# A scan's output product, made by the full array or by its four quarters

## The chip, the cores and the metric

The kernel runs on one core of a Trainium2 chip. The metric is the device time of one launch in microseconds (us), the median of several runs. A profile of one execution shows the engines: PE (matmul), PEld (its weight loads), DVE, ACT, POOL and SP (which here only issues DMAs).

## The reference

Four layers over an image x of 1024 channels and 64x64 places, each added to its input after a normalization over groups of channels:

```python
x = x + L0(gn(x))      # layernorm, decays from a softplus, a causal sum over channels
x = x + W1 @ gn(x) + b1
x = x + L2(gn(x))      # the scan layer
x = x + W3 @ gn(x) + b3
```

The change lies in the third layer. Its core is a selective scan over N = 4096 tokens in two heads, each with 512 channels and 8 states, each in an order of its own:

```python
perm = argsort(score of the token's place)              # one order per head
h_t = exp(dt_t * A) * h_{t-1} + dt_t * B_t * x_t        # 8 states x 512 channels
y_t = C_t . h_t + D * x_t
y = y put back into the order of the image
out = silu(Wo @ (y * silu(gate) + res))
```

## The kernel before

All arithmetic is f32. The large products (1024x1024 weights) are made by Strassen's method: sums and differences of blocks of the image (tiles t and b, lines 514 and 942) and of the weights (lines 471 to 495) are multiplied at line 984 into tiles mm.

The scan goes in chunks. A chunk holds both heads: partitions 0 to 63 are head 0, 64 to 127 head 1. Of the 64 rows of a head the first 8 are its states, the other 56 are tokens in scan order. So 74 chunks (NK) hold 4096 tokens. Token rows lie in DRAM (tok_d, 512 channels and 130 columns of dt, B and C). For chunk k:

- gather (line 1467, POOL): an indirect DMA brings 128 rows into rows[k] by the indices src, five chunks ahead.
- turn_rows (lines 1481 and 1482, PE): turns B, C and the sums of dt into the PSUM tile pr, one bank of the tag tp, which has two banks.
- spread_decay (lines 1488 to 1496, DVE): reads pr and makes the decays E and the operands cd and bts. Line 1496 is the last that reads pr.
- line 1560 (ACT): the exponential of E.
- cross (line 1503, PE): pg, the products of B and C. weigh (lines 1511 to 1516, DVE): from E and pg the matrix G, 128x128, of which only two diagonal blocks of 64x64, one for each head, are ever written; the rest is zero.
- apply (line 1520, PE): py = G^T rows[k], one product of 128x128 by 512 columns into the bank of tag y. Then ACT copies the 8 state rows of each head into the first rows of rows[k+1] (line 1523, two copies) and the whole of py over rows[k] (line 1525).
- scatter (line 1529, POOL): an indirect DMA writes the 128 rows of 512 channels to y_rows in DRAM by the indices dst. State rows and the rows beyond 4096 go to spare rows at the end.

In the same stage PE makes the products for res (line 984, function run), which lie between the steps of the scan: short steps hold 8 passes of them, long ones 16. ACT and DVE take their results from PSUM (lines 1173, 1177, 1185), ACT fills the image tiles for them (line 514), POOL makes differences of tiles (line 942) and sums of the last layer's weights.

The order of instructions on PE, DVE, ACT and POOL in this stage is that of the program (a manual schedule); only SP's order is left to the scheduler. The loop is:

```python
for k in range(-1, NK + 1):
    gather(k + 5); turned = turn_rows(k + 1); spread_decay(k + 1, *turned)
    next_units(upto)                 # products for res
    y = apply(k - 1); weigh(k, cross(k))
    exp(E of k + 1); step_sums(k + 3)
    scatter(k - 1, y)
    next_units(upto); next(sums)
```

The indices come from a sorting network that runs on DVE earlier, in the stage before (near 884 us). Its end (lines 402 to 414) writes the order to perm_d and reads it back, transposed, into src and dst, with POOL issuing the DMAs (lines 404, 410, 412). The rows of dst for states and spare rows are a constant, column "to", copied at line 232. After the scan, load_y (line 1677) reads y_rows for the output product.

Of the kernel before, what the change touches and what calls it, by code (L numbers as in the profile page):

```python
# [10 lines left out]
F32 = mybir.dt.float32  # L11
BF16 = mybir.dt.bfloat16
I32 = mybir.dt.int32
F32R = mybir.dt.float32r
AF = mybir.ActivationFunctionType
ALU = mybir.AluOpType
# [4 lines left out]
P = 128  # L21
C = 1024
HW = 64
N = HW * HW
CT = C // P
NB = 8
FB = N // NB
TPB = FB // P
NT = N // P
R = FB // HW  # L30
HEADS, S, DH = 2, 8, 512
# [4 lines left out]
LC = P // HEADS  # L36
# [38 lines left out]
        ("Alog", S), ("D", 1), ("mob", 4 * HEADS), ("dbcb", HEADS * NF)]  # L75

_CST = [("ident", P), ("fold", LC), ("same", P), ("upto", LC), ("far", LC), ("eye", LC), ("eye8", S),
        ("from", 1), ("to", NK), ("group", P), ("row", TR), ("rows", P),
        ("gx", NT), ("gy", NT), ("flip", 7)]


# [13 lines left out]
def tile_net(ctx: ExitStack, tc: tile.TileContext, x, par_d, cst_d, w_d, w2_d, dbcw_d, out):  # L95
# [19 lines left out]
    tok_d = dram.tile([HEADS * N + NSPEC, DH + NF2], F32, name="tok_d")  # L115
    y_d = nc.dram_tensor("y_rows", (HEADS * N + P * NK, DH), F32, kind="Internal").ap()
    perm_d = dram.tile([HEADS * N, 1], I32, name="perm_d")


    cst = const.tile([P, NCST], F32, name="cst")  # L120
# [102 lines left out]


    src = const.tile([P, NK], I32, name="src")
    dst_ = const.tile([P, NK], I32, name="dst")
    diag = const.tile([P, LC], F32, name="diag")

    def prepare_scan():

        nc.vector.tensor_copy(src, cst[:, CST["from"]].to_broadcast([P, NK]))
        nc.vector.tensor_copy(dst_, cst[:, CST["to"]])
        nc.vector.tensor_scalar(diag, cst[:, CST["eye"]], pcol("D", 0), None, ALU.mult)
        rows = sum1.tile([NSPEC, DH + NF2], F32, name="spec", bufs=1)
        nc.gpsimd.memset(rows, 0.0)
        for at in (BF, CF):
            for j in range(KW // HS)[HI[at]]:
                c = DH + at + j * HS
                nc.gpsimd.tensor_copy(rows[:HS, c : c + HS], ident[:HS, :HS])
        nc.sync.dma_start(tok_d[HEADS * N :, :], rows)  # L240
# [5 lines left out]
    turned_ = [sorts.tile([P, 2, HEADS * NT], F32, name=f"turned{i}") for i in range(2)]  # L246
    swap = [sorts.tile([P, 2, P // 2], F32, name=f"swap{i}") for i in range(2)]
    order_i = sorts.tile([HEADS * NT, P], I32, name="order_i")
    nc.gpsimd.iota(order_i, pattern=[[1, P]], base=0, channel_multiplier=P)

    def make_scores():
# [76 lines left out]
    def sort_work():  # L328

        eng, bits = nc.vector, 7
        flip = cst[: HEADS * NT, CST["flip"]]

        def compare(t, new, bit):
            def two(x):
                v = x.rearrange("p (u s l) -> p u s l", s=2, l=2 ** bit)
                return v[:, :, 0], v[:, :, 1]

            rows, _, w = t.shape
            a, b = two(t.rearrange("p c w -> p (c w)"))
            (ka, kb), (ia, ib) = two(t[:, 0]), two(t[:, 1])
            (ka2, kb2), (ia2, ib2) = two(new[:, 0]), two(new[:, 1])
            over = swap[0][:rows, :, : w // 2]
            same = swap[1][:rows, 0, : w // 2]
            step = swap[1][:rows, 1, : w // 2]
            def like(x):
                return x.rearrange("p (u l) -> p u l", l=2 ** bit)
            for i, (x, y) in enumerate(((ka, kb), (ia, ib))):  # L350
                eng.tensor_tensor(like(over[:, i]), x, y, ALU.is_gt)
            eng.tensor_tensor(like(same), ka, kb, ALU.is_equal)
            eng.tensor_tensor(same, same, over[:, 1], ALU.mult)
            eng.tensor_tensor(ka2, ka, kb, ALU.min)
            eng.tensor_tensor(same, same, over[:, 0], ALU.add)
            eng.tensor_tensor(like(step), ib, ia, ALU.subtract)
            eng.tensor_tensor(kb2, ka, kb, ALU.max)
            eng.tensor_tensor(step, step, same, ALU.mult)
            eng.tensor_tensor(ia2, ia, like(step), ALU.add)
            eng.tensor_tensor(ib2, ib, like(step), ALU.subtract)  # L360

        def negate(v):
            eng.tensor_scalar(v, v, -1.0, None, ALU.mult)

        def turn_over(t, new):
            rows, _, w = t.shape
            yield "turn"
            pt = ps_tp("sort")
            for c in range(2):
                nc.tensor.transpose(pt[:w, c * rows : (c + 1) * rows], t[:, c], ident[:rows, :rows])  # L370
            yield "take"
            nc.scalar.copy(new.rearrange("p c w -> p (c w)"), pt[:w, : 2 * rows])

        now, other = lines
        negate(now.rearrange("p c (u s l) -> p (c u) s l", s=2, l=2)[:, :, 1])
        for k in range(1, 13):
            if k > bits:
                t, t2 = turned_
                if k == bits + 2:
                    yield "take"  # L380
                yield from turn_over(now, t)
                for bit in reversed(range(k - bits)):
                    yield "compare"
                    compare(t, t2, bit)
                    t, t2 = t2, t
                yield from turn_over(t, now)
            for bit in reversed(range(min(k, bits))):
                yield "compare"
                compare(now, other, bit)
                now, other = other, now  # L390
            if k + 1 < bits:
                v = now.rearrange("p c (u t s l) -> p (c u) t s l", t=2, s=2, l=2 ** k)
                negate(v[:, :, 0, 1])
                negate(v[:, :, 1, 0])
            elif k + 1 == bits:
                v = now.rearrange("p c (s l) -> p c s l", s=2)
                for s in range(2):
                    eng.tensor_scalar(v[:, :, s], v[:, :, s], flip[:, s : s + 1], None, ALU.mult)
            elif k < 12:
                i = k - bits + 2  # L400
                eng.tensor_scalar(now, now, flip[:, i : i + 1], None, ALU.mult)
        eng.tensor_copy(order_i, now[:, 1])
        yield "take"
        nc.gpsimd.dma_start(perm_d.rearrange("(a p) o -> a (p o)", p=P), order_i)
        yield "take"
        for h in range(HEADS):
            r0, full = h * LC + S, (NK - 1) * LT
            perm = perm_d[h * N : (h + 1) * N]
            for idx in (src, dst_):
                nc.gpsimd.dma_start(idx[r0 : r0 + LT, : NK - 1],  # L410
                                  perm[:full].rearrange("(k r) o -> r (k o)", r=LT))
                nc.gpsimd.dma_start(idx[r0 : r0 + N - full, NK - 1 :], perm[full:])
# [1039 lines left out]
    with tc.tile_pool(name="l2g", bufs=8) as pgat, tc.tile_pool(name="l2b", bufs=2) as pb, tc.tile_pool(name="l2r2", bufs=4) as prg, tc.tile_pool(name="l2h", bufs=1) as ph, \  # L1452
# [7 lines left out]
        eye8 = cst[:KW, CST["eye8"]]  # L1460
        turn = cst[:, CST["ident"].start : CST["fold"].stop]
        rows, decay_, steps_ = {}, {}, {}
        y_views = dram_disjoint_views(y_d[:, :], 4)

        def gather(k):
            rows[k] = g = pgat.tile([P, DH + NF2], F32, tag="g", name=f"g{k}")
# [49 lines left out]
                nc.vector.tensor_tensor(G2[k % 2][at, at], K[at], diag[at], ALU.add)  # L1516

        def apply(k):
            py = psb.tile([P, FB], F32, tag="y", name=f"py{k}")
            nc.tensor.matmul(py, G2[k % 2], rows[k][:, :DH], start=True, stop=True)  # L1520
            if k + 1 < NK:
                for h in range(HEADS):
                    nc.scalar.copy(rows[k + 1][h * LC : h * LC + S, :DH], py[h * LC : h * LC + S])  # L1523
            y = rows.pop(k)[:, :DH]
            nc.scalar.copy(y, py)  # L1525
            return y

        def scatter(k, y):
            nc.gpsimd.indirect_dma_start(  # L1529
                out=y_views[k % len(y_views)][:, :], out_offset=bass.IndirectOffsetOnAxis(ap=dst_[:, k : k + 1], axis=0),  # L1530
                in_=y, in_offset=None,
            )

        sums = (None for _ in sum_weights2(W3, ph, nc.sync, 64, (2, 2, 1, 2, 1)))

# [396 lines left out]
def _constants():  # L1932
    c = np.zeros((P, NCST), np.float32)
    p, j = np.arange(P)[:, None], np.arange(P)[None, :]
    c[:, CST["ident"]] = p == j
    h, r = np.divmod(p, LC)
    t = np.arange(LC)[None, :]
    c[:, CST["fold"]] = r == t
    c[:, CST["same"]] = h == j // LC
    c[:, CST["upto"]] = (t < S) | (r <= t)  # L1940
    c[:, CST["far"]] = np.where((r >= S) & (t >= S) & (t < r), FAR, 0)
    c[:, CST["eye"]] = (r == t) & (r >= S)
    c[:KW, CST["eye8"]] = np.tile(np.eye(S), (KW // S, 1))
    c[:, CST["from"]] = HEADS * N + np.where(r < S, h * S + r, HEADS * S)
    c[:, CST["to"]] = HEADS * N + np.arange(NK)[None, :] * P + p
    c[:, CST["group"]] = (p // 32 == j // 32) / 32
    c[:, CST["row"]] = p // TW == j[:, :TR]
    c[:, CST["rows"]] = p % TR == j // TW
    s = 1 - 2 * ((np.arange(P)[:, None] >> np.arange(6)[None, :]) & 1)
    s[:, 5] = 1  # L1950
    c[:, CST["flip"]] = np.concatenate([s[:, :1], -s[:, :1], s[:, :5] * s[:, 1:]], axis=1)
    lin = _side()
    c[:, CST["gx"]] = np.tile(lin, HW).reshape(NT, P).T
    c[:, CST["gy"]] = np.repeat(lin, HW).reshape(NT, P).T
    return c
# [63 lines left out]
```

## Time and profile before

| | |
|---|---|
| time, median of 3 runs | 2605.09 us (2603.36 to 2606.09) |
| the profiled execution: its time | 2604.14 us |
| the profiled execution: its span | 2602.4 us, mean granted clock 0.998 |
| PE busy | 2539.4 us, 98% of the span |
| ACT busy, POOL busy | 1053.9 us and 1231.7 us |
| scan, first to last py (line 1520) | 1094.3 to 1536.5 us |
| py in the scan, PE | 148 passes, 592 ns each by their records |
| state copies, ACT, line 1523 | 146, median 576 ns |
| full copies, ACT, line 1525 | 74, median 585 ns |
| scatters, POOL, line 1529 | 74, median 996 ns |

The profile's line numbers are those of the kernel before. An f32 product appears as two passes, so its count is double. A pass's record reaches from its start to the modelled end of its drain, so records of passes that follow each other overlap; the pace is read from start to start. In a timeline each row is a run of equal instructions: start, length, engine, line, operation, out<-in, count. A number in brackets is the idle time of the engine before the row and what ended it.

### The profile page before, as it was taken

The numbers are of one execution on the slowest core, as the hardware profiler recorded it, in microseconds if no ns is written. First come the engines' busy times: TensorE is split into PE (matmuls) and PEld (weight loads), VectorE is DVE, ScalarE is ACT, GpSimd is POOL, SyncE is SP. The second block draws the span as 40 slices with busy tenths as digits, with TensorE's granted clock in tenths as the row PEclk, the third lists the DMA queues.
The fourth block names the chain that finished last, engine by engine and source line by source line (L and its number), as shares of the span: only waits on it lengthen the run. The fifth ranks groups of instructions, "written<-read, shape, count | busy, mean of one in ns | idle before, by whom it ended". The sixth has DMA issues, their size and how long they took to land.

```text
span 2602.4 us, 30961 instructions
## 1 busy us (share of the span) xinstructions
PE 2539.4 (98%) x9692; PEld 1681.3 (65%) x9692; DVE 1796.5 (69%) x3754; ACT 1053.9 (40%) x1829; POOL 1231.7 (47%) x1118
## 2 busy tenths in 40 slices
PE   5989999999999999999999999999999999899999
PEld 4654444445555555545454558888888888788887
DVE  7998675565556553487878866585685775877877
ACT  4871011025555644476767562243133323321120
POOL 4643332422424231355565636575564755655444
PEclk9999999999999999999999999999999999999999
DMA  7564747664755685587678847899898898888896
GB/s 284 214 231 154 267 168 229 206 208 127 213 136 139 145 216 142 186 283 232 207 213 256 280 157 202 224 303 271 244 304 245 240 301 226 301 287 303 299 319 216
DMA packets 426998, 597.26 MB, mean 230 GB/s; under 512 B 142004, under 2 KB 210739, under 8 KB 423764
## 3 DMA queue, kind: packets, MB, share of 16 engines
q1 hardware_dynamic: 307268, 384.69, 46.9%
q10 hardware_dynamic: 91744, 136.85, 15.0%
q0 software_dynamic: 27824, 73.74, 11.8%
q8 instruction: 79, 1.29, 0.2%
q14 instruction: 83, 0.68, 0.1%
HBM read 435.12 MB, written 160.05 MB: 229 GB/s over the span
## 4 chain that ended last, share of the span: by engine, by line
PE 85%; DVE 8%; ACT 4%; DMA 1%; issue 1%; POOL 1%; SPq 0%; ACTq 0%; DVEq 0%; POOLq 0%
PE mm L984 38%; PE q_P2P L1889 6%; PE q_P3P L1889 5%; PE q_P4P L1889 5%; PE q_P6P L1889 5%; PE q_P7P L1889 5%; PE q_P5P L1889 5%; PE q_P1P L1889 5%; PE l2pt L1235 2%; PE py L1520 2%; DVE xt L685 2%; ACT b L514 1%; DVE cvp L1216 1%; DVE stats L584 1%; PE pr L1481 1%
## 5 line engine op out<-in xcount | busy, mean ns | idle before, releaser
L984 PE MATMUL mm<-t,w 128*128 128x512 f32 x1504 | 667.5, 594 | 0.0
L984 PE MATMUL mm<-b,w 128*128 128x512 f32 x1088 | 483.1, 594 | 1.6 <-ACT xs L1259 1.1
L984 PEld LDWEIGHTS mm<-t,w 128*128 128x128 f32 x1504 | 279.7, 190 | 313.7 <-issue 305.5
L984 PEld LDWEIGHTS mm<-b,w 128*128 128x128 f32 x1088 | 202.4, 190 | 232.5 <-issue 225.4
L1529 POOL DMA_INDIRECT y_rows<-g,dst x74 | 73.6, 995 | 179.8 <-ACT g L1525 163.7
L1216 DVE SCALAR_TENSOR_TENSOR cvp<-xs,par,cvp 128x512 f32<-128x512 f32 x128 | 95.3, 754 | 76.4 <-ACT cvp L1213 74.1
L1853 ACT COPY qQ<-q_P5P 128x512 f32<-128x512 f32 x48 | 28.1, 585 | 295.7 <-PE q_P5P L1889 267.6
L471 POOL TENSOR_TENSOR s<-s 128x256 f32<-128x256 f32 (+3 forms) x120 | 130.3, 1091 | 7.5
L1523 ACT COPY g<-py 8x512 f32<-8x512 f32 x146 | 83.8, 574 | 104.0 <-PE py L1520 101.1
L1267 DVE TENSOR_TENSOR xs<-mm,xs 128x512 f32<-128x512 f32 x64 | 41.8, 685 | 118.2 <-PE mm L984 118.2
L1243 POOL TENSOR_TENSOR acc<-l2xt,acc 128x136 f32<-128x136 f32 x56 | 29.2, 522 | 194.2 <-ACT l2xt L1237 187.1
L1099 DVE SCALAR_TENSOR_TENSOR image<-mm,par,image 128x512 f32<-128x512 f32 x60 | 44.0, 745 | 84.3 <-PE mm L984 84.3
L1235 PEld LDWEIGHTS l2pt<-both,cv 128*128 128x128 f32 x512 | 76.2, 190 | 35.3 <-issue 21.5
L942 POOL TENSOR_TENSOR t<-t,b 128x512 f32<-128x512 f32 x36 | 49.5, 1401 | 96.0 <-DVE t L942 92.6
L1635 POOL TENSOR_TENSOR t_t<-qt 128x512 f32<-128x512 f32 x23 | 29.6, 1288 | 133.4 <-DVE qt L1635 68.8
L1639 ACT ACTIVATE qb<-x_x_b,gn_bias,gn_r_r 128x512 f32<-128x512 f32 x64 | 48.8, 808 | 107.8 <-DVE qQ L1813 37.3
L1889 PE MATMUL q_P4P<-t_t,wq_P4P 128*128 128x256 f32 x384 | 90.9, 380 | 1.4 <-DVE qV L1861 1.4
L1861 DVE TENSOR_TENSOR qV<-q_P4P,qV 128x512 f32<-128x512 f32 x96 | 64.8, 685 | 37.7 <-PE q_P4P L1889 36.0
L1889 PE MATMUL q_P5P<-t_t,wq_P5P 128*128 128x256 f32 x384 | 90.8, 379 | 0.0
L1889 PE MATMUL q_P6P<-t_t,wq_P6P 128*128 128x256 f32 x384 | 90.7, 379 | 0.0
L1889 PE MATMUL q_P7P<-t_t,wq_P7P 128*128 128x256 f32 x384 | 90.7, 379 | 0.0
L1889 PE MATMUL q_P2P<-t_b,wq_P2P 128*128 128x256 f32 x384 | 90.7, 379 | 0.0
(471 smaller groups left out, 5923.3 us busy)
## 6 DMA issues: line engine op xcount, KB each, us to landing
w<-s_d SPq DMA_DIRECT2D x96, 512.0 KB
w<-in_w_dram SPq DMA_DIRECT2D x70, 512.0 KB
x_x_b<-x_d ACTq DMA_DIRECT2D x28, 1024.0 KB
image<-x_d SPq DMA_DIRECT2D x12, 2048.0 KB
wq_P6P<-s_d SPq DMA_DIRECT2D x84, 256.0 KB
wq_P7P<-s_d SPq DMA_DIRECT2D x84, 256.0 KB
wq_P5P<-s_d SPq DMA_DIRECT2D x84, 256.0 KB
wq_P3P<-s_d SPq DMA_DIRECT2D x84, 256.0 KB
```

What stands on the lines that cost most here:

```text
L471: eng.tensor_tensor(out, a, b, ALU.subtract)
L685: nc.vector.tensor_tensor_scan(xt, spread[h].rearrange("p t c -> p (t c)"), xt, 0.0, ALU.mult, ALU.add)
L942: eng.tensor_tensor(B[name][k], B[one][k], B[two][k], ALU.subtract)
L984: nc.tensor.matmul(to[o], w[:, k, o * P : (o + 1) * P], B[name][k], start=(fresh and k == 0), stop=(k == KH - 1), skip_group_check=True)
L1216: nc.vector.scalar_tensor_tensor(cv, xo[:, at + t : at + t + FB], pcol("dww", 3 * o + t), cv, ALU.mult, ALU.add)
L1235: nc.tensor.matmul(pt[:, q * NV : (q + 1) * NV], cv[:, (q0 + q) * P : (q0 + q + 1) * P], both[:, o, :], start=True, stop=True)
L1520: nc.tensor.matmul(py, G2[k % 2], rows[k][:, :DH], start=True, stop=True)
L1523: nc.scalar.copy(rows[k + 1][h * LC : h * LC + S, :DH], py[h * LC : h * LC + S])
L1529: nc.gpsimd.indirect_dma_start(out=y_views[k % len(y_views)][:, :], out_offset=bass.IndirectOffsetOnAxis(ap=dst_[:, k : k + 1], axis=0), i ...
L1639: made = nc.scalar.activation(tile_of(j, name)[:, k], held[j, "x", name][:, k], AF.Identity, bias=bias, scale=scale)
L1861: nc.vector.tensor_tensor(to, ps, to, ALU.add)
L1889: nc.tensor.matmul(ps[:, o, :], w[:, k, o * P : (o + 1) * P], rhs[:, k, :], start=(new and o == 0 and k == 0), stop=(k == 1), skip_group_c ...
```

## The change

The product py becomes four. For each head h and each half of the channels (side) there is a product of the 64x64 block of G with 256 columns of that head's rows. The head decides which rows of the array it uses, the side decides which columns, so the four lie in the four quarters. Head 0's output goes to py[0], the bank of tag y, head 1's to py[1], a bank of tag tp; in each, partitions 0 to 63 hold the first 256 channels and 64 to 127 the other 256. The copies follow: four of 8x256 for the states, two of 128x256 for the whole. A row that is scattered is now half a token (256 channels), and each head is scattered by itself; the indices are 2*token + side, in DRAM tables of their own (sides_d), and the spare rows come from an iota.

```diff
-dst_ = const.tile([P, NK], I32, name="dst")
+dst_ = const.tile([P, HEADS, NK], I32, name="dst")
...
-nc.vector.tensor_copy(dst_, cst[:, CST["to"]])
+nc.gpsimd.iota(dst_, pattern=[[1, HEADS], [2 * P, NK]], base=2 * HEADS * N, channel_multiplier=2)
...
 nc.gpsimd.dma_start(perm_d.rearrange("(a p) o -> a (p o)", p=P), order_i)
+for i in range(2):
+    eng.tensor_scalar(side_i[i], now[:, 1], 2.0, float(i), ALU.mult, ALU.add)
+    nc.gpsimd.dma_start(sides_d[i].rearrange("(a p) o -> a (p o)", p=P), side_i[i])
 yield "take"
 for h in range(HEADS):
-    r0, full = h * LC + S, (NK - 1) * LT
-    perm = perm_d[h * N : (h + 1) * N]
-    for idx in (src, dst_):
+    full = (NK - 1) * LT
+    for idx, d, half in ((src, perm_d, h), (dst_[:, h], sides_d[0], 0), (dst_[:, h], sides_d[1], 1)):
+        r0 = half * LC + S
+        perm = d[h * N : (h + 1) * N]
         nc.gpsimd.dma_start(idx[r0 : r0 + LT, : NK - 1],
                           perm[:full].rearrange("(k r) o -> r (k o)", r=LT))
         nc.gpsimd.dma_start(idx[r0 : r0 + N - full, NK - 1 :], perm[full:])
...
-y_views = dram_disjoint_views(y_d[:, :], 4)
+y_views = dram_disjoint_views(y_d.rearrange("r (s c) -> (r s) c", s=2), 8)
...
 def apply(k):
-    py = psb.tile([P, FB], F32, tag="y", name=f"py{k}")
-    nc.tensor.matmul(py, G2[k % 2], rows[k][:, :DH], start=True, stop=True)
+    py = psb.tile([P, FB], F32, tag="y", name=f"py{k}"), ps_tp(f"py1_{k}")
+    for side in range(2):
+        to, at = slice(side * LC, (side + 1) * LC), slice(side * QB, (side + 1) * QB)
+        for h in range(HEADS):
+            own = slice(h * LC, (h + 1) * LC)
+            nc.tensor.matmul(py[h][to, :QB], G2[k % 2][own, own], rows[k][own, at], start=True, stop=True)
     if k + 1 < NK:
         for h in range(HEADS):
-            nc.scalar.copy(rows[k + 1][h * LC : h * LC + S, :DH], py[h * LC : h * LC + S])
+            for side in range(2):
+                nc.scalar.copy(rows[k + 1][h * LC : h * LC + S, side * QB : (side + 1) * QB],
+                               py[h][side * LC : side * LC + S, :QB])
     y = rows.pop(k)[:, :DH]
-    nc.scalar.copy(y, py)
+    for h in range(HEADS):
+        nc.scalar.copy(y[:, h * QB : (h + 1) * QB], py[h][:, :QB])
     return y

 def scatter(k, y):
-    nc.gpsimd.indirect_dma_start(
-        out=y_views[k % len(y_views)][:, :], out_offset=bass.IndirectOffsetOnAxis(ap=dst_[:, k : k + 1], axis=0),
-        in_=y, in_offset=None,
-    )
+    for h in range(HEADS):
+        nc.gpsimd.indirect_dma_start(
+            out=y_views[(HEADS * k + h) % len(y_views)][:, :],
+            out_offset=bass.IndirectOffsetOnAxis(ap=dst_[:, h, k : k + 1], axis=0),
+            in_=y[:, h * QB : (h + 1) * QB], in_offset=None,
+        )
```

The column "to" is also gone from the constants, which shrink from 954 to 880 columns. In the order of instructions nothing else moves on PE, DVE, ACT and POOL: each py, each copy and each scatter is replaced where it stood. On SP one weight load goes ahead of the three stores that preceded it.

## The prediction

> **What bounds the kernel now.** I read the page first, then windows over the stage that the change touches, the waits of PE there, and the timelines of PE, DVE and ACT inside it. The page gives the whole:
>
> ```profile
> span 2602.4 us, 30961 instructions
> PE 2539.4 (98%) x9692; PEld 1681.3 (65%) x9692; DVE 1796.5 (69%) x3754; ACT 1053.9 (40%) x1829; POOL 1231.7 (47%) x1118
> ```
>
> PE is the bound on average; what a change in one stage is worth depends on the stage. The scan's 74 steps run from 1094 to 1540 us. A window inside it, and the waits of PE over it (total, times, longest, us):
>
> ```profile
> 1150.00:1200.00 50.00, 50.00 (x144) 25.15 (x142) 38.67 (x87) 31.61 (x57) 37.58 (x36) 1.00 0.73 223
> ...
> PE py L1520 <- DVE G L1516: 2.3, 3, 1.5
> PE py L1520 <- ACT g L1525: 1.6, 2, 1.4
> ```
>
> PE never stops (50.00 of 50.00, full clock); its few waits are all for this product. So PE time removed here is span removed, as long as nobody else becomes late. The timeline of PE shows one short step:
>
> ```profile
> 1320.36 1.02 PE L1520 MATMUL py<-g,G 128*128 128x512 f32 x2
> 1320.82 0.80 PE L1503 MATMUL pg<-cd,bts 66*128 66x512 f32 x1
> 1321.46 0.49 PE L1481 MATMUL pr<-cst,g 128*128 128x192 f32 x2
> 1321.79 0.33 PE L1482 MATMUL pr<-ds,cst 128*128 128x64 f32 x2
> 1321.95 3.65 PE L984 MATMUL mm<-t,w 128*128 128x512 f32 x8
> 1325.44 1.02 PE L1520 MATMUL py<-g,G 128*128 128x512 f32 x2
> ```
>
> An f32 product is two passes (x2). Records overlap, so I take start to start: a pass of 512 columns occupies PE 0.427 us (eight mm passes: 3.49, from 1321.95 to 1325.44, the first with its weights not yet loaded), so py occupies 0.854 of the 5.08 us step. 256 columns are then 0.213 a pass.
>
> **The change on PE.** Removed: 74 py of 2 passes x 0.427 = 0.854. Added: four products of 2 passes x 0.213, which is 1.71 in a row, 0.43 if all four quarters run at once. The kernel has a near relative: line 642 puts four f32 products of 256 columns side by side in four column strips.
>
> ```profile
> 64.23 1.14 PE L626 MATMUL xpt<-cst,xn 128*128 128x128 f32 x8
> 65.30 0.64 PE L642 MATMUL pd<-xt,dtm 128*32 128x256 f32 x8
> 65.86 1.13 PE L704 MATMUL pb<-image,cst 128*128 128x512 f32 x2
> ```
>
> Eight passes start and are gone in 0.56 (65.30 to 65.86), not 1.71: four do run at once. But there is a toll. The L626 passes come every 0.122 ((1.14 - 0.286)/7, 0.286 being one record), so they end at 65.21 and L642 enters 0.09 late; and the pair behind takes 1.13 where a pair in stride takes 1.02. The visit costs 0.09 + 0.56 + 0.11 = 0.77 (0.785 in most of the others), that is 0.43 of work and 0.35 of toll. The Trainium skill, "TensorEngine Tiling (Array Packing)", Key Properties, says that changing the tiling mode drains TensorE, without a figure. The same toll for a split by rows:
>
> ```profile
> 358.26 2.31 PE L984 MATMUL mm<-t,w 128*128 128x512 f32 x5
> 360.50 0.34 PE L370 MATMUL sort<-cst,lines 64*128 64x64 f32 x2
> 360.76 2.41 PE L984 MATMUL mm<-t,w 128*128 128x512 f32 x5
> ```
>
> Five passes are 2.14, so 2.50 from 358.26 to 360.76 holds 0.36 of the visit, and the 2.41 behind it (2.31 in stride) 0.10 more: 0.46 for 0.107 of work. Both kinds of split cost 0.35, so I take 0.785 for the py visit; the bounds are 0.75 and 0.85 (weights of 64 columns instead of 32). By the skill's speedup of up to four (Theoretical Speedup, same page) the sum would be 74 x (0.43 - 0.854) = -31 us; with the drain in the trace it is 74 x (0.785 - 0.854) = -5.1 us. In some ten steps PE waits at py anyway, for ACT or DVE, so 64 steps give **-4.4 us** (bounds -6.5 and 0).
>
> **ACT.** Before: two copies 8x512 and one 128x512 per step; after: four 8x256 and two 128x256. The nearest row of half width from PSUM stands last:
>
> ```profile
> 1110.38 1.50 ACT L514 ACTIVATE b<-image,gn2b_bias,gn2b_r_r 128x512 f32<-128x512 f32 x2
> 1111.79 1.15 ACT L1523 COPY g<-py 8x512 f32<-8x512 f32 x2
> 1112.96 0.58 ACT L1525 COPY g<-py 128x512 f32<-128x512 f32 x1
> ...
> L647 ACT COPY own<-pd 128x256 f32<-128x256 f32 x8 | 3.0, 379 | 1.2 <-PE pd L642 1.2
> ```
>
> Half the columns save a third only: 4 x 0.37 + 0.38 + 0.27 (the last overlaps its follower by 0.1, as now) = 2.13 against 1.68 = +0.43 us per step, 32 us in all on an ACT that is busy 312 of 446 us. In most steps py(k) comes 2.2 us after the end of the full copy L1525 of k-1, which hides it. It is not hidden where fills (L514) or activations stand ahead of the copies in ACT's queue: the starts of py at 1113.60, 1124.10, 1259.07 and 1392.28 follow the end of L1525 within 0.06; there +0.43 each. At 1240.06 and 1373.26 ACT has worked without a pause over two or three steps; there about +1.1 each. Sum 1.7 + 2.2 = **+3.9 us** (bounds 2 and 6). E (exp) comes 0.43 later too; DVE reads it 3 us afterwards.
>
> **A new wait, pr for DVE.** Head 1's output takes a bank of tag tp, which until now alternated between the pr of two steps. Now pr(k+1) always gets the bank of pr(k), and the order of instructions shows it: pr waits for DVE, which it didn't before. It must wait until line 1496, the last reader of pr(k), is done; mm, py and all else on PE queue behind it.
>
> ```profile
> 1320.54 0.67 DVE L1496 TENSOR_TENSOR cd<-pr,cst 64x512 fp32r<-64x512 f32 x1
> ...
> 1144.94 0.67 DVE L1496 TENSOR_TENSOR cd<-pr,cst 64x512 fp32r<-64x512 f32 x1
> ...
> 1144.64 0.49 PE L1481 MATMUL pr<-cst,g 128*128 128x192 f32 x2
> ```
>
> In the usual short step L1496 ends at 1321.21 and pr starts at 1321.46: 0.25 us of slack, as in nearly thirty steps. A released PE instruction starts 0.05 after the release with 0.105 of weight load uncovered (a 1.13 py behind a wait against 1.02), so 0.16 are needed and 0.18 are left once py is 0.07 shorter: no stall. But where DVE is behind, pr now starts before L1496 ends: by 0.97 at 1144.64 and 0.98 at 1279.06, 0.34 at 1210.78, 0.13 at 1095.79, 0.5 at 1133.81, 0.39 at 1284.14. Adding 0.16 gives 1.1, 1.1, 0.5, 0.3, 0.66, 0.55. The fifth only shortens the wait for G at 1143.47, the last is gone since PE is then 1.1 later and DVE has caught up. With a little for two slacks of 0.1: **+3.3 us** (bounds 1.5 and 6).
>
> **POOL and DMA.** A second scatter per step, 0.995 each: +74 us on a POOL that is busy 243 of 446 and waits 164 for ACT before scatters. Behind it in the queue stand the gathers (five steps ahead) and the differences L942 for mm; of the tightest pair, ended at 1307.15, the product begins at 1311.80 and needs the second half 2.6 us later, so 7 us of slack hide 1.4 to 3. Without that cover a late difference would stop PE by about 1.4 a time, twelve sets. The second scatter also waits for the gather two steps back; its tail is at most 9 us behind the issue, two steps are 10. The bytes are the same in rows of 1 KB instead of 2: between nothing and twice the packet time of the scatters (half of the 28% that the software queue holds of the 16 engines here); no wait of PE in this stage ends at a DMA, so I take nothing. Before the scan: two writes of the sides (0.78 each), two more index pairs (1.9 + 0.54 each), 6.5 us on POOL at 884 to 902, ahead of weight sums and acc; POOL then idles 3.5 and 3.2 us, so 0 to 3 us come through. The two DVE multiplications (near 0.2, the row of the cast L402), the iota (0.23, row L249) against the dropped cast (0.19), and 74 columns less of constants: nothing, each being paid once and for a quarter of a microsecond. Rearranged on SP: one weight load ahead of three stores; nothing. Together **+1.0 us** (0 to 4).
>
> **Sum.** -4.4 + 3.9 + 3.3 + 1.0 = +3.8 us on the profiled execution (span 2602.4, own time 2604.14, 1.7 outside the span). The median of the runs is 2605.09, one above it: 2609.
>
> **Rivals.** *B, two rounds.* The Trainium skill, "TensorE: Matmul & The Clock Gate", Part 3 (What overlaps and what doesn't), says that a weight load overlaps running products only in another row group. The two halves of one head share a row group; they would run after each other: 2 x 0.427 + 0.35 = 1.21 per visit, +0.35 x 74 = +26, the new waits then covered by the slower PE: 2632. Against: the strips of L642 share all rows and yet all eight passes fit in 0.56. *C, no packing:* the quarters aren't used at once: 1.71 + 0.35, +1.2 x 74 = +89 less some cover: 2690. Nothing in the trace speaks for it but that quarters of 64x64 are not shown. *D, the cover fails:* POOL or DMA waits reach PE, +8 to +20: 2618. *E, faster:* the drain isn't paid for quarters, because G and the products are ready early and the queue is full: the visit falls to 0.48, -27 + 8 = -19: 2586. For it: L370 in 128*64 form enters and leaves without a toll (five passes and the visit take 2.36 from 406.79 to 409.15). Against: that one has all rows and starts at column 0, and both true splits pay. The turn to faster than before lies at a visit of 0.73.
>
> **How the numbers follow.** Main case 0.78 (2602 to 2616), B 0.08, C 0.05, D 0.04, E 0.05. About 0.2%, 5.2 us, is what a measurement of this kernel can tell from no change. The main case lies around +4 with a spread of 3, so it splits into 0.42 same, 0.35 slower, 0.01 faster; B, C, D are slower, E is faster: 0.06, 0.42, 0.52. The range reaches from 2602 over D to 2622, leaving out B, C, E.
>
> **What would show it.** Right: py as 64*64 passes, eight in 0.64 and a step near 5.0; py's visit 0.78; ACT copies of 0.36 to 0.38; waits of pr for DVE near 1144 and 1279; longer py waits for ACT near 1240 and 1373. Wrong: eight passes in 1.0 or more, short steps over 5.1, or PE waits that end at POOL or a DMA.

## The result, and the profile after

The changed kernel is slower: 2621.24 us (median of 5 executions, 2620.56 to 2630.48) against 2605.09 us for the kernel before on the same chip, ratio 1.0073 with a 95% interval of 1.0062 to 1.0084. The forecast was 2609. Nine executions of it were timed in all: seven lie between 2617.8 and 2621.6 us, two at 2629.9 and 2630.5. The first profile is one of these two; where not said otherwise, the lines below are from a profile of the same kernel at 2617.8 us, taken on the chip of the second group of experiments, where before had 2605.48 us. Line numbers are those of each run's own kernel.

```profile
span 2616.0 us, 32307 instructions
...
PE 2539.8 (97%) x10136; PEld 1667.4 (64%) x10136; DVE 1797.4 (69%) x3755; ACT 1080.6 (41%) x2049; POOL 1308.8 (50%) x1199
```

PE is as busy as before (2539.4 then) in a span that is 13.6 us longer: PE does not work more, it stands still more. To find where, I followed the start of the k-th pg in both timelines. Three stretches come out:

| stretch | before | after, 2617.8 us | longer by |
|---|---|---|---|
| start to first pg | 1090.08 | 1099.64 | 9.6 |
| first pg to last pg (scan) | 441.89 | 444.41 | 2.5 |
| last pg to end of span | 1070.4 | 1072.0 | 1.6 |

The scan is where the change is, and it lost 2.5 us. Nearly four times that was lost before it begins. One short step of the scan, in the timeline of PE:

```profile
1296.73 0.66 PE L1530 MATMUL py<-g,G 64*64 64x256 f32 x8
1297.32 0.50 PE L1509 MATMUL pg<-cd,bts 66*128 66x512 f32 x1
1297.66 0.49 PE L1487 MATMUL pr<-cst,g 128*128 128x192 f32 x2
1297.99 0.33 PE L1488 MATMUL pr<-ds,cst 128*128 128x64 f32 x2
1298.15 3.65 PE L990 MATMUL mm<-b,w 128*128 128x512 f32 x8
1301.74 0.66 PE L1530 MATMUL py<-g,G 64*64 64x256 f32 x8
```

The eight passes of the four quarters (x8 in the first line) stand in a record of 0.66 us, and pg starts 0.59 after the first of them: the quarters do run at once. The step is 1301.74 - 1296.73 = 5.01 us against 5.08. Between py and mm 0.17 us is gained (1.42 against 1.59), and 0.10 is given back at the switch from mm to py (3.59 against 3.49): 0.07 in all, as forecast. The waits of PE from 1090 to 1556 us (total, times, longest):

```profile
PE py L1530 <- ACT g L1538: 3.4, 6, 1.6
PE pr L1487 <- issue: 2.3, 2, 1.2
PE pr L1488 <- ACT ds L1481: 1.3, 3, 0.6
PE py L1530 <- ACT rg L1191: 1.3, 1, 1.3
PE pr L1487 <- PE pg L1509: 1.1, 3, 0.5
```

No line ends at POOL or a DMA. The waits of pr are new, and so are two of the three for ds (what ACT makes for pr's second product), which stands behind the copies in ACT's queue; the third, 0.6 at 1092.30, lies ahead of the first pg and has its like in the kernel before. The two pr lines are one wait: the profile puts it down to "issue" or to the pg just ahead, but at 1155.85 pr starts 0.11 us after the last reader of the earlier pr on DVE ends (1155.07 + 0.67 = 1155.74):

```profile
1155.85 0.56 PE L1487 MATMUL pr<-cst,g 128*128 128x192 f32 x2 [1.10 <-issue]
...
1155.07 0.67 DVE L1502 TENSOR_TENSOR cd<-pr,cst 64x512 fp32r<-64x512 f32 x1
```

Before the scan, the chain that ended last runs, for the first time, through the index work. Each line is start, length and what was waited for:

```profile
883.69 6.59 DMA perm_d<-order_i
890.57 1.95 POOL src L416
893.08 1.90 POOL dst L416
895.51 1.89 POOL dst L416
897.93 1.79 issue
899.72 1.90 POOL src L416
902.15 2.52 issue
904.67 1.90 POOL dst L416
...
911.33 1.42 POOL s L477 x2
914.55 2.43 DMA s_d<-s
...
928.79 10.43 DMA tok_d<-l2xt
939.80 2.53 PE l2pt L1241 x8
```

Read it downward: six pairs of index loads on POOL, then POOL's weight sums (s), SP's stores of these (s_d), then the token store (tok_d from l2xt), which stands behind them on SP, and behind loads that wait until they have landed; ACT waits for that store before it can refill l2xt, and PE waits for ACT. In the kernel before, the same view of the same stretch has no POOL line at all. But it has this:

```profile
920.88 0.64 ACT l2xt L1237 x2
921.52 0.31 ACT cvp L1213
921.83 10.43 DMA tok_d<-l2xt
932.36 0.76 ACT l2xt L1237 x2
```

The token store, with the same 10.43 us, was on the chain already. It had no slack; SP now hands it over 7.0 us later, and all of that arrives (l2pt starts at 939.80, its like before at 932.84). The windows on both sides of it (before first, then after; behind the length stands PE's busy time, and the column that reads 1.00 or 0.61 is the granted clock of TensorE):

```profile
932.00:942.00 10.00, 8.96 (x31) 5.08 (x32) 6.67 (x12) 5.64 (x12) 4.27 (x3) 1.00 0.76 184
942.00:952.00 10.00, 10.00 (x36) 5.65 (x35) 0.26 (x1) 2.79 (x6) 4.65 (x6) 1.00 0.78 199
```

```profile
932.00:942.00 10.00, 2.20 (x8) 2.20 (x9) 1.17 (x2) 2.14 (x4) 2.05 (x4) 0.61 1.10 344
942.00:952.00 10.00, 10.00 (x32) 5.46 (x31) 7.66 (x11) 3.78 (x8) 6.68 (x6) 0.88 0.64 165
```

PE works 2.20 us of ten, the clock is halved while it stands, and stays so for some 4.6 us after it has resumed (934.2 to 944.4 us), which costs an estimated 2.3 us more (half of 4.6). Two l2pt further on (951.25, before 942.48), 8.8 of the 9.6 us are there; I did not trace the rest.

### The profile page after: what moved, and what is told of

Read it like the earlier page. It is cut to its first block, busy times and chain, and to the rows that moved or that the text cites. A ratio compares the mean times of both kernels' runs of the same rounds, so it can differ in the third digit from the quotient of the medians.

```text
span 2627.6 us, 32307 instructions
## 1 busy us (share of the span) xinstructions
PE 2544.9 (97%) x10136; PEld 1669.5 (64%) x10136; DVE 1796.2 (68%) x3755; ACT 1080.5 (41%) x2049; POOL 1309.1 (50%) x1199
## 4 chain that ended last, share of the span: by engine, by line
PE 83%; DVE 8%; ACT 4%; DMA 2%; POOL 2%; issue 2%; SPq 0%; DVEq 0%; ACTq 0%; POOLq 0%
PE mm L990 36%; PE q_P2P L1904 6%; PE q_P3P L1904 5%; PE q_P5P L1904 5%; PE q_P4P L1904 5%; PE q_P6P L1904 5%; PE q_P7P L1904 5%; PE q_P1P L1904 5%; PE l2pt L1241 2%; DVE xt L691 2%; PE py L1530 1%; PE pg L1509 1%; PE pr L1487 1%; DVE cvp L1222 1%; DVE stats L590 1%
## 5 line engine op out<-in xcount | busy, mean ns | idle before, releaser
L1543 POOL DMA_INDIRECT y_rows<-g,dst x148 | 144.1, 974 | 124.9 <-ACT g L1538 90.6
L1534 ACT COPY g<-py 8x256 f32<-8x256 f32 x292 | 105.5, 361 | 86.2 <-PE py L1530 53.3
L1241 PE MATMUL l2pt<-both,cv 128*128 128x162 f32 x512 | 82.9, 306 | 12.0 <-ACT l2xt L1243 11.8
L1517 DVE TENSOR_TENSOR E<-E,pg 128x512 f32<-128x512 f32 x74 | 50.6, 683 | 61.7 <-PE pg L1509 38.6
```

What stands on the lines that cost most here:

```text
L1241: nc.tensor.matmul(pt[:, q * NV : (q + 1) * NV], cv[:, (q0 + q) * P : (q0 + q + 1) * P], both[:, o, :], start=True, stop=True)
L1517: nc.vector.tensor_tensor(Ef, Ef, pg, ALU.mult)
L1534: nc.scalar.copy(rows[k + 1][h * LC : h * LC + S, side * QB : (side + 1) * QB], py[h][side * LC : side * LC + S, :QB])
L1543: nc.gpsimd.indirect_dma_start(out=y_views[(HEADS * k + h) % len(y_views)][:, :], out_offset=bass.IndirectOffsetOnAxis(ap=dst_[:, h, k : k ...
```

## Experiments

Theory 1 says that the index work delays the start of the scan through POOL and SP. Theory 2 says that pr's new wait for DVE is what the scan loses. The rivals are ACT's split copies, the second scatter, and a scan that suffers only because it starts late. Each run was timed beside the kernel before on the same chip.

**The index work alone.** The kernel before, with this added, a third tile that nothing reads, and the constant "to" replaced by an iota as in the change:

```diff
+for i in range(2):
+    eng.tensor_scalar(side_i[i], now[:, 1], 2.0, float(i), ALU.mult, ALU.add)
+    nc.gpsimd.dma_start(sides_d[i]..., side_i[i])
...
-    for idx in (src, dst_):
+    for idx, d in ((src, perm_d), (dst_, perm_d), (extra_ix, sides_d[1])):
+        perm = d[h * N : (h + 1) * N]
```

> The kernel before, with only the index work of the change put in: two scaled copies of the sorted order are written to DRAM beside the first, and a third pair of index loads is issued on POOL (into a tile that nothing reads). Product, copies and scatter stay as before. Theory 1 (the later start of the scan comes from this: POOL is about 9 us later with its weight sums, SP's queue waits for POOL's blocks and hands the token stores over 8 us later, and PE stands still for them at 940 us): first pg 11 to 12 us later than before (1101.9 against 1090.1), scan of unchanged length, time +10 to +13 us. Rival (the start of the scan moved for another reason, such as the planner's order or the clock): first pg within 2 us, time within 3 us of before.

Measured: 2615.74 us against 2605.77 (ratio 1.0038, 1.0024 to 1.0052), so +10.0. The first pg is at 1100.14 and the scan lasts 441.88 us, to 0.01 us that of before. The product, the copies and the scatter are those of before, and yet PE stands still at the same place:

```profile
939.41 2.53 PE L1241 MATMUL l2pt<-both,cv 128*128 128x162 f32 x8 [9.42 <-ACT l2xt L1243]
```

Theory 1 is right in mechanism and size.

**The changed kernel without the added index work.** The permutation goes to DRAM once, four pairs of loads bring it into both halves of the destination tile, and the rest is made from it on DVE ahead of the scan (the part on DVE):

```diff
+            for h in range(HEADS):
+                half = slice(h * LC, (h + 1) * LC)
+                nc.vector.tensor_scalar(src[half], dst_[half, h], cst[half, CST["from"]], None, ALU.min)
+            for side in range(2):
+                half = dst_[side * LC : (side + 1) * LC].rearrange("p h k -> p (h k)")
+                nc.vector.tensor_scalar(half, half, 2.0, float(side), ALU.mult, ALU.add)
```

> The changed kernel with its index work cut back to before: the permutation alone is written to DRAM and four pairs of loads bring it into both halves of the destination tile; the source indices and the doubled destinations are made from that on DVE by four small operations ahead of the scan. Theory 1: first pg back at 1090 to 1092, time about 11 us under the changed kernel, 2608 to 2611; the scan keeps its 11.7 us of extra length. Rival (the scan's loss is a follow-up of the late start, through another alignment of the clock and of the transfers): the scan also comes back, time near 2600. Second rival (the start has another cause): time stays at 2619 to 2622.

Measured: 2608.84 us (1.0011, 1.0002 to 1.0019). First pg at 1091.29, scan 444.47 us. The time is the expected one, but one part of what I expected was wrong: the scan does not keep 11.7 us of extra length. That length came from the first profile, one of the two long executions; this scan loses 2.6.

**The changed kernel once more,** without an edit, to see an execution of the lower group.

> The changed kernel once more, without an edit, because its five times fall into two groups (2620.6 to 2621.2, and 2629.9 and 2630.5, of which the profile is one). Theory (the late start costs 11.8 us in every run; the scan itself loses only the 2.6 us that the kernel with four index loads showed; the rest of the profiled execution are two windows of half clock at steps 32 and 54 and stalls around them): a profile of the lower group has its first pg again at 1101.9, shows no half clock between 1102 and 1555 us, and its scan from the first pg to the last is 444.5 to 446 us, not 453.6. Rival (the scan's stalls are there in every run, and the two groups differ elsewhere): scan near 453 us in it too.

Measured: 2618.54 us (1.0055, 1.0038 to 1.0072), first pg 1099.64, no half clock in the scan, scan 444.41 us. The start is 2.2 us earlier than in the first profile; otherwise as expected. The table above is from this run.

**The same loads in another place.** Nothing is removed: the four pairs into dst_ are only issued after the last weight sum of the stage.

```diff
-    for idx, d, half in ((src, perm_d, h), (dst_[:, h], sides_d[0], 0), (dst_[:, h], sides_d[1], 1)):
+    load_index(src, perm_d, h, h)
...
             for _ in sums:
                 pass
+            for h in range(HEADS):
+                for half in range(2):
+                    load_index(dst_[:, h], sides_d[half], h, half)
```

> The changed kernel with the same index loads, but with the four pairs into the destination tile issued on POOL after the last weight sum of the stage (where POOL stands idle from about 1018 to 1040 us), not ahead of the weight sums at 893 us. Nothing is removed. Theory 1 (what counts is the place: POOL's index loads stand ahead of the weight sums, SP's queue waits for those, and the token stores behind them hold up ACT and PE): PE's stand at 940 us gone, first pg at 1088 to 1093, time 2606 to 2611. Rival (the loads themselves, their many small packets or their number, cost what they cost wherever they stand): first pg at 1098 or later, time 2616 or more.

Measured: 2607.03 us (1.0005, 0.9997 to 1.0014). The first pg is at 1088.34, earlier than before, and PE no longer waits for l2xt at all:

```profile
926.88 1.26 PE L1242 MATMUL l2pt<-both,cv 128*128 128x162 f32 x8
927.98 3.60 PE L991 MATMUL mm<-t,w 128*128 128x512 f32 x8
931.41 1.26 PE L1242 MATMUL l2pt<-both,cv 128*128 128x162 f32 x8
```

In the kernel before, four pairs stood ahead of the sums and PE waited 0.17, 1.29 and 0.20 us here; now two pairs stand there, and that is gone too. It is the place in POOL's queue that costs, not the loads, which now run from 1006.65 to 1016.33 us. The profiled scan lasted 446.07 us, 1.6 of it a half clock (see the end).

**The token stores on ACT's queue** instead of SP's, with the index work as changed:

```diff
-nc.sync.dma_start(tok_rows(t0, TPB, P, c0, h), xt)
+nc.scalar.dma_start(tok_rows(t0, TPB, P, c0, h), xt)
```

(and the two stores of the first block likewise)

> The changed kernel with its token stores (tok_d from l2xt) issued on ACT's queue, not on SP's; the index work stays as changed. Theory (the index work reaches PE only through SP's queue, where the token stores stand behind the block stores that wait for POOL): PE no longer stands still for l2xt at 940 us, first pg at 1091 to 1095, time 2609 to 2614. Rival (the index work reaches PE by another way as well, a late weight load or the gathers behind POOL's issues): first pg at 1099 or later, time above 2617.

Measured: 2620.73 us (1.0059, 1.0042 to 1.0076), first pg 1104.49. A miss: the order on SP is not the only way. ACT's own issue of the store was held up (the idle time before each in brackets):

```profile
931.82 0.45 ACTq L1255 DMA_DIRECT2D tok_d<-l2xt  x1
932.32 1.33 ACT L1274 ACTIVATE xs<-xs,par 128x512 f32<-128x512 f32 x2 [9.88 <-DMA s_d<-s]
```

ACT stood 9.88 us. The semaphores in the trace show for what: ahead of the token store ACT waits for the semaphore on which the last of SP's four block stores (s_d, issued at 928.21) tells of its landing, and the token store uses the same one for its own. ACT goes on at 931.77; SP, which waits for it too, at 931.76. In the trace of the changed kernel the token store shares a semaphore with the last block store (922.08) as well. So there are two ties to POOL's sums, the order on SP and the shared semaphore, and this run, which cuts only the first, cannot tell what each is worth. PE was also 5.6 us late at 884 us already, ahead of the index loads. That the place of the loads is the cause rests on the chain and on the run with the loads moved.

**pr's wait alone.** The kernel before with one edit:

```diff
-py = psb.tile([P, FB], F32, tag="y", name=f"py{k}")
+py = ps_tp(f"py{k}")
```

> The kernel before, with one word changed: the output product py takes its bank from the rotation of two that pr uses, not from a tag of its own. Product, copies, scatter and order of instructions are the same; what is added is that pr must wait for the last DVE reader of the pr one step earlier, as in the changed kernel. Theory 2 (this wait is the largest part of what the scan lost, with stalls of PE up to 2.4 us at single steps and a half clock after some): time +5 to +9 us, with starts of pr 0.1 us after the end of the cd multiply at the steps 9, 11, 22, 33, 45 and 55. Rival (the wait only takes up idle time that PE would have elsewhere, and the ACT copies or the array's forms are what costs): within 2 us of before.

Measured: 2608.08 us (1.0010, 1.0002 to 1.0019), +2.3; scan 444.53 us, +2.6. The waits are where they were expected, and no half clock follows. From 1090 to 1535 us:

```profile
PE pr L1481 <- PE pg L1503: 2.6, 4, 0.9
PE py L1520 <- DVE G L1516: 1.8, 2, 1.5
```

Theory 2 has the place right; its size of 5 to 9 us came from the long execution and falls. The wait also absorbs others, as the prediction had it: step 8 gets 0.68 us longer and step 9 0.67 shorter, and step 25 gives 0.60 back.

**ACT's split alone.** The kernel before with its copies cut in two by columns:

```diff
-nc.scalar.copy(y, py)
+for side in range(2):
+    half = slice(side * QB, (side + 1) * QB)
+    nc.scalar.copy(y[:, half], py[:, half])
```

(and the state copies likewise)

> The kernel before, with its two state copies of 512 columns cut into four of 256 and its full copy into two of 256 columns, as in the changed kernel; nothing else. Theory (ACT's share, 3.9 us in the prediction, about 2 us in the trace of the changed kernel): +1.5 to +4.5 us, with waits of py for ACT at the same steps. Rival (ACT is what the scan lost): +8 us or more.

Measured: 2608.15 us (1.0012, 1.0004 to 1.0020). The scan takes 443.65 us, +1.8, in seven steps of 0.17 to 0.51. As expected; the rival falls. (The first pg of this profile is 2.3 us late, in code that is not touched; single executions differ by that much.)

**One scatter in place of two,** on the kernel with four index loads:

```diff
-            for h in range(HEADS):
-                nc.gpsimd.indirect_dma_start(
-                    out=y_views[(HEADS * k + h) % len(y_views)][:, :],
...
+            nc.gpsimd.indirect_dma_start(
+                out=y_views[k % len(y_views)][:, :], out_offset=bass.IndirectOffsetOnAxis(ap=dst_[:, 0, k : k + 1], axis=0),
```

> The kernel with four index loads and one scatter of 128 rows of 512 per step in place of two of 128 rows of 256. The rows go to the places of the kernel before while the product still lays them out by quarters, so that the scattered rows are mixed between halves; the amounts are those of before. Theory (the second scatter is hidden, as the prediction said: no wait of PE on POOL or a DMA in the scan): within 1 us of the kernel with four index loads, 2607.8 to 2609.8. Rival (the second scatter delays the gathers or POOL's sums and so PE): 2606 or less.

The rows then land mixed between the halves; their bytes are those of before. Measured: 2609.18 us (1.0016, 1.0009 to 1.0023), scan 444.41, against 2608.84 and 444.47 with two, each beside the kernel before on its own chip (+4.0 and +3.1). 74 scatters of 1 us on POOL are hidden.

**Releasing pr earlier.** Three runs. In the first two, cd goes ahead of the decay and D moves to SBUF, so that pr's last reader ends some 0.65 us sooner:

```diff
 nc.vector.tensor_copy(bts[:KW], BC[KW:, :P])
+nc.vector.tensor_tensor(cd[:KW], BC[:KW, P:]..., eye8..., ALU.mult)
+E = decay_[k] = pb.tile([P, S, LC], F32, tag="E", name=f"E{k}")
+D = E[:, S - 1]
...
```

> The kernel with four index loads, in which DVE also leaves pr sooner: the cd multiply (reads pr) goes ahead of the decay, and D is kept in SBUF (in the last part of E), so that the decay's multiply no longer reads pr. The last reader of pr ends about 0.65 us sooner each step. Theory 2 (pr's waits for DVE are about 2 to 3 us of that scan): the stalls of 0.3 to 1.3 us ahead of pr at steps 3, 9, 11, 22 and 33 shrink by up to 0.65 each, scan 442 to 443.5 us, time 2606 to 2608 against 2608.8. Rival (stalls of that size only move to the product's wait for G or for ACT): time unchanged within 1 us.

> The kernel before with the same earlier end of pr's reads on DVE (cd ahead of the decay, D in SBUF); product, copies, scatter and index work as before. It is the counterpart of the kernel with four index loads and early reads. Theory (in the kernel before nothing waits for pr's readers, since pr has two banks of its own): within 1 us of before. Rival (an earlier cd lets the cross product start sooner and shortens steps): 2 us or more below before.

With four index loads: 2606.02 us (1.0001, 0.9992 to 1.0009), scan 441.83, as expected or a little better. On the kernel before: 2615.45 us (1.0038, 1.0024 to 1.0053), +10, which neither side expected. Timelines of DVE, POOL and PE in that run:

```profile
1421.27 5.82 DVE L1497 TENSOR_TENSOR E<-E,negA 128x512 f32<-128x512 f32 x1
...
1421.60 4.94 POOL L942 TENSOR_TENSOR t<-b,t 128x512 f32<-128x512 f32 x4
...
1429.39 2.04 PE L1521 MATMUL py<-g,G 128*128 128x512 f32 x2 [2.87 <-DVE G L1517]
```

A multiply of 0.69 us takes 5.82 while POOL runs four sums of 4.94 us in all, and G, py and PE are late after it. TensorE then runs at half clock from 1428.87 for two intervals of 3.413 us, which is why the two passes of py take 2.04; an estimated 3 of the 10 us (half of the time that PE works in them) are this. All 16 multiplies of this run that take over 0.8 us overlap sums of POOL. To tell this from the new order, cd alone was moved, with D left in PSUM:

> The kernel before, with the cd multiply moved ahead of the decay on DVE, and D left in PSUM. It takes apart the run of before with early reads (2615.5), which moved cd and put D into SBUF. Theory (there the loss comes from the decay's multiply, which with both operands in SBUF takes 1089 ns on average and up to 5.8 us while POOL works, against 691 ns with D in PSUM): here the multiply is back at 690 ns, and the time within 1.5 us of before. Rival (the loss comes from the order, cd ahead of the decay): 2610 or more.

Measured: 2605.53 us (1.0002, 0.9994 to 1.0010). The group of the multiply, first with D in SBUF, then with D in PSUM (busy, mean ns):

```profile
L1497 DVE TENSOR_TENSOR E<-E,negA 128x512 f32<-128x512 f32 x72 | 78.4, 1089 | 2.5
```

```profile
L1496 DVE TENSOR_TENSOR E<-pr,negA 128x512 f32<-128x512 f32 x72 | 49.8, 692 | 2.4
```

The order costs nothing; the operand in SBUF does, in the kernel before. The Trainium skill, "SBUF — State Buffer", section on SBUF's two separate sides, says that of a DVE operation with two SBUF inputs and a GpSimd operation that reads SBUF, the one that starts first has the port for its whole instruction and the other waits. The rows agree that DVE waits, but not on who goes first: the multiply's record begins 0.33 us ahead of POOL's first sum (1421.27 and 1421.60), and it is held up through all four. The slow multiplies are in the changed kernels too: with four index loads their mean is 916 ns and the longest 3.58 us, and that kernel still gains. Which steps they fall on differs; why they stay off PE's path there was not traced.

**Both mends together:** destination loads behind the weight sums, pr released early.

> The changed kernel with the destination loads moved behind the weight sums and with the earlier end of pr's reads on DVE (cd first, D in SBUF): the version that the runs so far point to. Theory: the start of the scan as in the kernel before, the scan 441 to 443 us; time 2603 to 2607, level with before within what can be told. Rival (the decay's multiply, with both operands in SBUF, is held up by POOL's sums at other steps than in the run with four index loads): 2608 to 2615.

Measured: 2602.33 us against 2605.23, ratio 0.9993, interval 0.9985 to 1.0001. First pg 1088.30, scan 441.72. It is the fastest version here, some 19 us under the changed kernel's first median (on another chip), but its interval just includes the kernel before: level, with a hint of better.

## Why the prediction was wrong, and where it was right

**The step that failed is "Before the scan", the last part of POOL and DMA.** It put 6.5 us of index work on POOL, saw that "POOL then idles 3.5 and 3.2 us", and let 0 to 3 us come through. What came through was 9.6 us, and 10.0 with the index work alone; it had no term for the half clock behind the stall either. Three errors stand in that sentence:

- Idle time was taken for slack. Those very pauses, in the kernel before:

```profile
908.96 1.13 POOL L495 TENSOR_TENSOR s<-s 128x448 f32<-128x448 f32 x1 [3.53 <-DMA s_d<-s]
...
917.60 0.77 POOL L1243 TENSOR_TENSOR acc<-l2xt,acc 128x136 f32<-128x136 f32 x1 [3.21 <-ACT l2xt L1237]
```

  The first waits for SP's store of the sum that POOL has just made. If POOL is later, so is that store: the pause moves along and absorbs nothing. The second does absorb, but too late: it lies behind the sums whose stores hold up SP. In the changed kernel the first is as long as before and the second is gone:

```profile
917.11 1.31 POOL L501 TENSOR_TENSOR s<-s 128x448 f32<-128x448 f32 x1 [3.56 <-DMA s_d<-s]
...
922.01 1.03 POOL L1249 TENSOR_TENSOR acc<-l2xt,acc 128x136 f32<-128x136 f32 x2
```

- The next queue was not followed. SP stands at its first block store until POOL is done, and has the token stores and the weight loads behind it. It stood there up to 15.0 us in one piece before, and 18.1 now:

```profile
SPq L492 <- POOL s L471: 16.2, 2, 15.0
...
SPq L498 <- POOL s L477: 18.1, 1, 18.1
```

  Whether these have slack is read in the chain of the kernel before, which went through the token store at 921.83. I read that chain only inside the scan.
- The loads were priced at their issue time. From the permutation's store to the first weight sum, POOL took 884.41 to 902.40 = 18.0 us before and 883.69 to 910.45 = 26.8 after: 8.8 more, of which 4.3 are pauses between the pairs (1.79, 2.52 and 0.93 in the chain and timeline, against 0.99) that no count of instructions shows.

**PE's visit was right:** 0.785 forecast; measured 5.01 - (5.08 - 0.854) = 0.784. The 31 us that a visit without toll would save (the page named there has a factor of up to two for a dimension of 64, so four for both) do not come. In the scan nearly all steps without a stall are 0.05 to 0.08 shorter, together -4.0 us against -4.4 (what is left of the 2.5 when the jumps below, and 0.23 in the first step that I did not trace, are taken off). Rivals B and C, which had the quarters run in two rounds or singly, and E, which had no toll, are out by the same rows.

**pr's wait was near:** +3.3 forecast; +2.6 alone in the kernel before, and in the changed kernel the longer steps at 2, 8, 10, 21, 32 and 54, less step 9, add up to 3.8 (0.31 + 0.68 + 1.27 + 0.62 + 1.33 + 0.34 - 0.75). Its places were right: 0.31 near 1096, 1.27 near 1145, 0.62 near 1211 and 1.33 near 1279, and what came near 1134 was given back at once, as it had it (0.68, then -0.75).

**ACT was too high in one part and lacked another.** Forecast +3.9; six steps of py gave 0.20, 0.20, 0.72, 0.20, 0.42 and 0.20 = 1.9 (0.38 of the 0.72 is a wait for ds, at 1247.02). The copies are as long as forecast (361 and 376 ns), but two things shorten the wait: head 0's product needs only the first of the two full copies, whose bank it takes, and the copies start 0.71 us after py where they started 1.06 after it. What the forecast lacked is ds, which is behind the copies on ACT and held up pr's second product by 0.38 us at step 14. An ACT_TABLE_LOAD of 1.28 us, which the kernel before has in the same step, stands between the two there:

```profile
1178.05 1.28 ACT L1575 ACT_TABLE_LOAD   x1
...
1180.27 0.43 PE L1488 MATMUL pr<-ds,cst 128*128 128x64 f32 x2 [0.38 <-ACT ds L1481]
```

That step is 0.58 longer; ACT has 2.5 in all.

**The sum in the scan** was -4.4 + 3.9 + 3.3 = +2.8, and 2.5 was measured: right, with errors that partly cancel. With the index loads out of the way, the kernel that keeps the four quarters runs at 2607.0 or 2608.8 us. Rival D had its size (+8 to +20) but looked for it in the scan's scatters and differences, where the cover held. That 2621 still lies inside the range up to 2622, which was drawn to take in D, is luck.

**The second scatter** was hidden, as forecast.

Open: the last 1.6 us after the scan, which lie within what single executions differ by, and the two executions at 2630. The profile of one of these has 453.6 us of scan, with two half-clock intervals and waits that it puts down to no engine and no DMA of this core (it calls them remote); no other profile has such lines:

```profile
1287.65 0.29 DVE L1494 CAST bts<-pr 64x128 fp32r<-64x128 f32 x1 [1.30 <-remote]
...
1421.88 0.75 ACT L1534 COPY g<-py 8x256 f32<-8x256 f32 x2 [1.40 <-remote]
```

## What to carry to other kernels

An engine's idle time is slack only if what it waits for does not depend on the engine itself, and only if it lies ahead of what others wait for: follow the work that you add through every queue behind it, to the first instruction on the path that sets the end, and look in the chain of waits whether that path already passes there. A change to a loop body brings preparation with it; cost the preparation in its own stage and put it where its queue is idle, as moving four pairs of loads by some 110 us did here for more than 11 us. A tiling of TensorE that halves the product's own time, 0.85 to 0.43 us, gained 0.07 us of a 5.08 us step, because entering and leaving it cost 0.35.

## What the hardware showed that I had not expected

The clock of TensorE dropped to half for intervals of 3.413 us, on a raster that is fixed within an execution, after PE had stood still inside one interval of it. (In the first profile they begin at 935.20, 1297.01 and 1436.96 us, 106 and 41 intervals apart.) It is not a matter of one long pause: the same wait of py for ACT, 1.64 us, cost nothing at 1252.58 in the profile at 2617.8 us, and in the run with late loads at 1241.27 it was followed by a whole interval at half clock:

```profile
1241.27 0.76 PE L1534 MATMUL py<-g,G 64*64 64x256 f32 x8 [1.64 <-ACT g L1542]
...
1242.30 5.29 PE L991 MATMUL mm<-t,w 128*128 128x512 f32 x8
```

The eight passes take 5.29 us where they take 3.65, and that step is 1.63 longer. The first wait lay across two intervals of the raster, the second inside one. That alone doesn't decide it: in the first profile the same wait, ended at 1255.61, lay inside one interval and brought no drop, idle sums of 1.65 and 1.85 us within one interval also went by without a drop, and the two of 2.2 and 2.4 us in the scans both brought one. The Trainium skill, "TensorE: Matmul & The Clock Gate", Part 1, has the free-running window of 3413 ns, and asks for about a whole idle window before the clock falls; here less than half of one was enough in some executions (1.64 us in the run with late loads, 1.31 in the first profile, ahead of 1297.01). Such a wait costs its own length and sometimes 1.7 us more.
